# Conditional mix, attention and routed feed-forward on one core: conditions of the first tile by register loads, the routed matrix by the whole array, another load order, a gate sum ahead of a scaling, and the last product in 384 + 128 columns

## The chip, the cores and the metric

The kernel runs on one core of one Trainium2 chip. The metric is device time in microseconds (us) of one execution, the median of several runs. All data are float32 except the integer conditions and adapter numbers.

## The reference

The input `x` is 128 sequences of 32 tokens of 512 numbers. Per sequence:

```python
W  = cond_weights[condition]                  # 32x32, one of 16, chosen per sequence
h  = einsum('bct,bcd->bdt', x, W)             # mixes the 32 tokens
q, k, v = split(clip(h @ w_qkv.T, -8, 8))     # layer norm on q and on k
a  = softmax(q k^T / 4 + alibi, causal) v     # 32 heads of 16
x  = x + a @ w_out.T
u  = x @ weight[adapter].T                    # 512x512, one of 8, chosen per sequence
gate = sum(top2(u @ gate_w))                  # one number per token
y  = relu(u @ up_w)**2 @ down_w + gate * (u @ fc1_w @ expert_w @ fc2_w)
out = x + layernorm(y) * gamma + beta
```

The product `fc1_w @ expert_w @ fc2_w` does not depend on `x`.

## The kernel before, in words

Four sequences make a tile of 128 rows, so there are 32 tiles (`NTILE`). Everything is one program written out in order; a scheduler places it on the five engines, and each engine then works through its own list in order. `after(a, b)` (L130) only fixes that `a` stands behind `b`, without a wait of its own. Each DMA queue (SP's, ACT's, GpSimd's) is also worked through in order. The steps of the first tiles are written out by hand (L603 to L708); from tile 2 on a loop (L716) runs the steps of several tiles interleaved: `weigh` of tile t, `scores` of t + 1, `mix` and `project` of t + 2, and the feed-forward of the pair before.

The start. 14 products of a tile of ones (`idle`, L118 to L122) have no use but to keep TensorE busy. The conditions are loaded spread over 128 partitions (`cond_b`, L81), VectorE makes row numbers of them (`rows`, L92), and `load(t)` (L176) loads the tile `x_t` on SP's queue and gathers its condition weights `cw` row by row by an indirect DMA of GpSimd (L182). `blend` (L230) spreads `cw` into a block diagonal 128 x 128 matrix `blk` on GpSimd (L234), `mix` (L241) multiplies `x_t` with it on TensorE (`pxc`, L246), and ScalarE evicts to `xcT`. `project` (L253) multiplies `xcT` with the q, k and v weights (`wqkv_sb`, L263), which SP loads in twelve pieces (L607).

The routed matrix. `routed_inner` (L148) makes `e2 = expert @ fc2` in two halves (`pe`, L151), and `routed_outer(c)` (L157) multiplies with `fc1` into `rout_sb`, a quarter at a time. Its weights are 32 columns wide, so that four products stand side by side in the array (`pro`, L161). `rout_sb` is laid out so that partition 32 g + d of quarter c stands for row 128 g + 32 c + d.

Attention. `normalise` (L278) scales q and k on VectorE (L282), `share` (L394) divides the softmax on GpSimd (L400), `flip` (L404) transposes it to `pT` on VectorE (L408), and `weigh` (L430) multiplies `pT` with the spread values (`po`, L434). `turn_x` (L460) adds `beta` on GpSimd (L468). One line in `flip` puts the transposition of tile 2 behind the last scaling of tile 3.

Feed-forward. `load_adapters` (L192) reads the adapter numbers of a tile into registers of SP and loads its adapter weights by them (L210), `adapt` multiplies (`pad`, L484). `route` (L496) makes the gate's numbers and the routed output (`pr`, L503); VectorE takes the eight largest (`top`, L510) and adds the first two (`gs`, L512), and ScalarE scales by `gs` (L514). `up` and `down` are the feed-forward proper (L523, L537). For the very last tile `close` (L566) takes their place: it multiplies with `down_w` in two halves of 256 columns (L576), adds each half and takes its statistics on VectorE (L580, L583), then normalises and stores.

Of the kernel before, what the change touches and what calls it, by code (L numbers as in the profile page):

```python
# [11 lines left out]
F32 = mybir.dt.float32  # L12
I32 = mybir.dt.int32
AF = mybir.ActivationFunctionType
ALU = mybir.AluOpType
# [26 lines left out]
def adaln_attn_ffn(  # L42
# [27 lines left out]
    def bank(name):  # L70
        return ps.tile([P, 512], F32, tag="ps", name=name)
# [6 lines left out]


    cond_b = const.tile([P, NTILE], I32, name="cond_b")  # L80
    nc.sync.dma_start(  # L81
        out=cond_b, in_=cond.unsqueeze(1).broadcast_to([SEQ, S, NTILE])
    )
    msk = const.tile([P, SEQ + HC], F32, name="msk")
    nc.scalar.dma_start(out=msk, in_=masks)
    chan = const.tile([P, NTILE], I32, name="chan")
    for j in range(SEQ):
# [1 line left out]
            chan[j * S : (j + 1) * S, :], pattern=[[0, NTILE]], base=0, channel_multiplier=1  # L89
        )  # L90
    rows = const.tile([P, NTILE], I32, name="rows")
    nc.vector.scalar_tensor_tensor(  # L92
        out=rows, in0=cond_b, scalar=float(S), in1=chan, op0=ALU.mult, op1=ALU.add
    )
    m_seq = msk[:, 0:SEQ]
    ids = const.tile([1, B], I32, name="ids")
    wqkv_sb = const.tile([P, DC, 3 * D], F32, name="wqkv_sb")
# [20 lines left out]
    idle = hp.tile([P, GRP * P], F32, tag="act", name="idle")[:, :P]  # L118
    nc.vector.memset(idle, 1.0)
    pi = bank("pi")  # L120
    for i in range(14):
        nc.tensor.matmul(pi[:, :P], lhsT=idle, rhs=idle, start=True, stop=True)  # L122


# [11 lines left out]
        )  # L136


    exp_t = wp.tile([P, LC, LAT], F32, tag="adw", name="exp_t")
    nc.scalar.dma_start(out=exp_t, in_=expertT.rearrange("(c p) f -> p c f", p=P))  # L140
    fc2_t = wp.tile([P, LC, D], F32, tag="adw", name="fc2_t")
# [2 lines left out]
    fc1_dma = nc.sync.dma_start(out=fc1_t, in_=fc1T.rearrange("(c p) f -> p c f", p=P))  # L144
    after(fc1_dma, fc2_dma)
    e2 = w2.tile([P, LC, D], F32, tag="hT2", name="e2")

    def routed_inner(l):  # L148
        pe2 = bank(f"pe2_{l}")
# [7 lines left out]
    def routed_outer(c):  # L157
        pro = bank(f"pro_{c}")
        for l in range(LC):
            for g in range(DC):  # L160
                nc.tensor.matmul(  # L161
                    pro[ts(g, S), :],
                    lhsT=fc1_t[:, l, g * P + c * S : g * P + (c + 1) * S], rhs=e2[:, l, :],
                    start=(l == 0), stop=(l == LC - 1),
                )
        nc.scalar.copy(rout_sb[:, c, NE:], pro)

    def rstd_of(mv, n, name):
# [7 lines left out]
    def load(t):  # L176
        x_t = xp.tile([P, D], F32, tag="x", name=f"x_{t}")
        dma = nc.sync.dma_start(out=x_t, in_=x[ts(t, P), :])
        if t == 0:
            after(dma, fc1_dma)  # L180
        cw = sm.tile([P, S], F32, tag="cw", name=f"cw_{t}")
        nc.gpsimd.indirect_dma_start(  # L182
            out=cw,
            out_offset=None,
            in_=cond_w,
            in_offset=bass.IndirectOffsetOnAxis(ap=rows[:, t : t + 1], axis=0),
        )
        tiles[t] = {"x": x_t, "cw": cw}

    last_adapter_dma = []  # L190

# [38 lines left out]
    def blend(t):  # L230

        s = tiles[t]
        s["blk"] = w2.tile([P, SEQ, S], F32, tag="blk", name=f"blk_{t}")
        nc.gpsimd.tensor_tensor(  # L234
            out=s["blk"],
            in0=s["cw"].unsqueeze(1).broadcast_to([P, SEQ, S]),
            in1=m_seq.unsqueeze(2).broadcast_to([P, SEQ, S]),
            op=ALU.mult,
        )
# [38 lines left out]
    def normalise(t):  # L278
        s = tiles[t]
        r = rstd_of(s["mv"], 2, f"qk_{t}")  # L280
        for i in range(2):
            s["done"] = nc.vector.tensor_scalar(  # L282
                out=s["qk"][:, i, :], in0=s["qk"][:, i, :],
                scalar1=s["mv"][:, i, 0:1], scalar2=r[:, i : i + 1],
                op0=ALU.subtract, op1=ALU.mult,
            )

    last_flip = []
    last_pad = []
# [114 lines left out]
    def flip(t):  # L404

        s = tiles[t]
        s["pT"] = w1.tile([P, H, S], F32, tag="pT", name=f"pT_{t}")
        pT = nc.vector.transpose(  # L408
            out=s["pT"].rearrange("p h q -> p (h q)"),
            in_=s["s"].rearrange("p h k -> p (h k)"),  # L410
        )
        if t == GRP:
            after(pT, tiles[t + 1]["done"])

    def spread(t):

# [79 lines left out]
    def route(t, half):  # L496

        s = tiles[t]
        hT = pairs[t // GRP]["hT"]
        n = ROUT[half + 1] - ROUT[half]  # L500
        pr = bank(f"pr_{t}_{half}")
        for c in range(DC):
            nc.tensor.matmul(  # L503
                pr[:, :n], lhsT=hT[:, c, ts(t % GRP, P)],
                rhs=rout_sb[:, c, ROUT[half] : ROUT[half + 1]],
                start=(c == 0), stop=(c == DC - 1),
            )
        if half == 0:
            top = sm.tile([P, 8], F32, tag="top", name=f"top_{t}")
            nc.vector.max(out=top, in_=pr[:, :NE])  # L510
            s["gs"] = sm.tile([P, 1], F32, tag="gs", name=f"gs_{t}")
            nc.vector.tensor_tensor(out=s["gs"], in0=top[:, 0:1], in1=top[:, 1:2], op=ALU.add)  # L512
# [53 lines left out]
    def close(t):  # L566

        s = tiles.pop(t)
        y, n = s["y"], D // 2
        banks = [bank(f"pd_{t}_{h}") for h in range(2)]  # L570
        st = sm.tile([P, H], F32, tag="mx", name=f"stf_{t}")[:, :12].rearrange(
            "p (h n) -> p h n", h=2
        )
        for h in range(2):
            for f in range(FC):
                nc.tensor.matmul(  # L576
                    banks[h][:, :n], lhsT=pairs[t // GRP]["acts"][f][:, ts(t % GRP, P)],
                    rhs=down_sb[:, f, ts(h, n)], start=(f == 0), stop=(f == FC - 1),
                )
            nc.vector.tensor_tensor(  # L580
                out=y[:, ts(h, n)], in0=y[:, ts(h, n)], in1=banks[h][:, :n], op=ALU.add
            )
            nc.vector.bn_stats(out=st[:, h], in_=y[:, ts(h, n)])  # L583
        mv = sm.tile([P, 1, 2], F32, tag="mv1", name=f"mvf_{t}")
        nc.vector.bn_aggr(out=mv[:, 0, :], in_=st)
        r = rstd_of(mv, 1, f"f_{t}")
        for h in range(2):
            nc.vector.scalar_tensor_tensor(
                out=y[:, ts(h, n)], in0=y[:, ts(h, n)], scalar=mv[:, 0, 0:1],
                in1=gam_sb[:, ts(h, n)], op0=ALU.subtract, op1=ALU.mult,  # L590
            )
        for h in range(2):
            nc.vector.scalar_tensor_tensor(
                out=y[:, ts(h, n)], in0=y[:, ts(h, n)], scalar=r,
                in1=s["x"][:, ts(h, n)], op0=ALU.mult, op1=ALU.add,
            )
            (nc.sync, nc.scalar)[h].dma_start(
                out=out[ts(t, P), ts(h, n)], in_=y[:, ts(h, n)]
            )

    load(0)  # L603
    for cols in ((0, 1), (2,)):
        for c in range(DC):
            for i in cols:
                dma = nc.sync.dma_start(  # L607
                    out=wqkv_sb[:, c, ts(i, D)], in_=w_qkvT[c * P : (c + 1) * P, ts(i, D)]
                )
                after(dma, fc1_dma)  # L610
    load(1)
    for l in range(LC):
        routed_inner(l)
    blend(0)
    blend(1)
    mix(0)
    routed_outer(0)
# [222 lines left out]
```

## Time and profile before

| | us |
|---|---|
| median of 3 runs (1243.22 to 1243.87) | 1243.75 |
| the profiled execution, whole | 1243.48 |
| its span, first to last instruction | 1241.7 |
| busy: GpSimd (POOL) | 431.3 |
| busy: ScalarE (ACT) | 327.6 |
| matmuls of the q, k, v products (L263), 768 records | 340.3 |
| matmuls of the routed matrix (L151 and L161), 8 and 64 records | 3.7 and 7.5 |
| matmuls of the last product (L576), 32 records | 7.1 |
| matmuls of ones (L122), 28 records | 5.3 |

One execution is profiled, and times in it count from its first instruction. An engine's busy time is the union of its instructions; a matmul's end is modelled, so that consecutive ones overlap. Each float32 matmul stands as two records. PE is TensorE's multiplication, PEld its weight load, DVE is VectorE, ACT is ScalarE, POOL is GpSimd, SP issues DMAs; a q behind an engine's name is its queue of instructions that only issue or wait. In a line such as `pxc L246 <- POOL blk L234` the engine's instruction on line 246 waited for GpSimd's on line 234.

### The profile page before, as it was taken

What the parts mean: (1) busy time and instruction counts of PE and PEld (TensorE: products, weight loads), DVE (VectorE), ACT (ScalarE), POOL (GpSimd) and SP (SyncE); (2) the same over time, 40 slices, a digit from 0 to 9 for tenths busy, and PEclk for the clock granted to TensorE, in tenths of its full rate; (3) what the DMA queues carried; (4) which work ended last, traced back from release to release, by engine and by line L of the source; (5) the groups of instructions that cost most, each with busy time, mean ns of one, the idle gap of its engine ahead of it and who ended that gap; (6) DMA issues with size and microseconds to landing.
All of it is one profiled execution on the core that took longest, in us unless ns stands there. A gap on an engine that the chain in (4) does not pass through costs nothing.

```text
span 1241.7 us, 28016 instructions
## 1 busy us (share of the span) xinstructions
PE 1231.8 (99%) x11676; PEld 793.6 (64%) x11676; DVE 656.8 (53%) x1086; ACT 327.6 (26%) x648; POOL 431.3 (35%) x393
## 2 busy tenths in 40 slices
PE   9999999999999999999999999999999999999997
PEld 5476566674666756567665666746667565675765
DVE  2874654646456364563645546465564646636222
ACT  2433223222222313233132232222322222231211
POOL 4444333333433424234243333333333242342410
PEclk9999999999999999999999999999999999999999
DMA  9745554435545355543445444455353554533620
GB/s 312 212 163 188 204 194 149 152 122 204 205 160 169 117 178 196 184 175 135 146 180 205 180 153 136 147 204 204 141 177 108 189 204 169 181 113 143 214 109 18
DMA packets 93380, 209.23 MB, mean 169 GB/s; under 512 B 11717, under 2 KB 42438, under 8 KB 93254
## 3 DMA queue, kind: packets, MB, share of 16 engines
q1 hardware_dynamic: 89270, 198.65, 45.8%
q0 software_dynamic: 3424, 8.39, 1.9%
q8 instruction: 92, 1.51, 0.5%
q10 hardware_dynamic: 560, 0.40, 0.1%
q14 instruction: 34, 0.28, 0.1%
HBM read 176.47 MB, written 30.93 MB: 167 GB/s over the span
## 4 chain that ended last, share of the span: by engine, by line
PE 97%; DVE 1%; DMA 1%; issue 0%; POOL 0%; SPq 0%; DVEq 0%
PE pqkv L263 26%; PE pu L523 18%; PE pd L537 17%; PE pr L503 9%; PE pad L484 9%; PE pw L454 9%; PE psc L366 3%; PE po L434 3%; PE pxc L246 2%; PE pro L161 1%; PE pd L576 1%; DMA adw<-in_adapt_w 0%; DVE qk L282 0%; POOL cw L182 0%; PE pt L317 0%
## 5 line engine op out<-in xcount | busy, mean ns | idle before, releaser
L263 PE MATMUL pqkv<-wqkv_sb,xcT 128*128 128x512 f32 x768 | 340.3, 592 | 0.0
L263 PEld LDWEIGHTS pqkv<-wqkv_sb,xcT 128*128 128x128 f32 x768 | 145.3, 190 | 169.1 <-issue 162.9
L523 PE MATMUL pu<-hT,up_sb 128*128 128x256 f32 x1024 | 228.7, 379 | 0.0
L537 PE MATMUL pd<-down_sb,act 128*128 128x512 f32 x496 | 220.4, 592 | 0.0
L523 PEld LDWEIGHTS pu<-hT,up_sb 128*128 128x128 f32 x1024 | 193.5, 190 | 32.6 <-issue 6.9
L342 DVE TENSOR_TENSOR kx<-T_qk,m_half 128x512 f32<-128x512 f32 x128 | 107.4, 897 | 106.5 <-ACT T_qk L338 106.5
L537 PEld LDWEIGHTS pd<-down_sb,act 128*128 128x128 f32 x496 | 93.2, 190 | 104.7 <-issue 103.6
L421 POOL TENSOR_TENSOR vx<-v,msk 128x1024 f32<-128x1024 f32 x64 | 126.7, 2004 | 60.4 <-DVE v L269 49.9
L529 POOL TENSOR_TENSOR act<-act 128x256 f32<-128x256 f32 x128 | 78.1, 615 | 166.7 <-ACT act L528 165.7
L503 PE MATMUL pr<-rout_sb,hT 128*128 128x256 f32 (+1 forms) x512 | 125.8, 389 | 0.0
L484 PE MATMUL pad<-adw,T_x 128*32 128x128 f32 x4096 | 119.9, 273 | 0.5 <-issue 0.4
L387 POOL TENSOR_TENSOR s<-s,mx 128x1024 f32<-128x1024 f32 x32 | 61.2, 1914 | 157.0 <-DVE top L510 146.2
L454 PE MATMUL pw<-wout_sb,aT 128*128 128x512 f32 x256 | 115.2, 592 | 0.0
L503 PEld LDWEIGHTS pr<-rout_sb,hT 128*128 128x128 f32 x512 | 94.7, 190 | 32.0 <-issue 19.9
L484 PEld LDWEIGHTS pad<-adw,T_x 128*32 128x32 f32 x4096 | 111.4, 110 | 3.3 <-issue 2.1
L397 DVE TENSOR_REDUCE den<-s 128x32 f32<-128x1024 f32 x32 | 39.0, 1220 | 100.5 <-ACT s L392 97.0
L468 POOL TENSOR_TENSOR x<-x,bet_sb 128x512 f32<-128x512 f32 x32 | 40.9, 1279 | 144.8 <-DVE blocks_x L298 144.8
L454 PEld LDWEIGHTS pw<-wout_sb,aT 128*128 128x128 f32 x256 | 48.6, 190 | 60.6 <-issue 60.0
L528 ACT ACTIVATE act<-pu 128x256 f32<-128x256 f32 x128 | 47.2, 379 | 140.9 <-PE pu L523 140.9
L564 POOL DMA_DIRECT2D out<-y x30 | 18.0, 601 | 180.2 <-DVE y L560 93.1
L400 POOL TENSOR_TENSOR s<-s,rden 128x1024 f32<-128x1024 f32 x32 | 61.5, 1921 | 50.7 <-DVE rden L399 47.8
L251 ACT COPY xcT<-pxc 128x512 f32<-128x512 f32 x32 | 18.7, 585 | 201.6 <-PE pxc L246 200.2
(75 smaller groups left out, 1100.5 us busy)
## 6 DMA issues: line engine op xcount, KB each, us to landing
adw<-in_adapt_w SPq DMA_DIRECT2D x256, 512.0 KB
away_qk<-blocks_qk SPq DMA_DIRECT2D x28, 512.0 KB
T_qk<-away_qk SPq DMA_DIRECT2D x112, 128.0 KB
x<-in_x SPq DMA_DIRECT2D x32, 256.0 KB
away_x<-blocks_x SPq DMA_DIRECT2D x30, 256.0 KB
T_x<-away_x SPq DMA_DIRECT2D x120, 64.0 KB
out<-y POOLq DMA_DIRECT2D x30, 256.0 KB, 2.9
wqkv_sb<-in_w_qkvT SPq DMA_DIRECT2D x12, 256.0 KB
```

Source lines behind the costliest of these rows:

```text
L263: nc.tensor.matmul(s["pp", i], lhsT=s["xcT"][:, c, :], rhs=wqkv_sb[:, c, ts(i, D)], start=(c == 0), stop=(c == DC - 1),)
L342: kx = nc.vector.tensor_tensor(out=s["kx"][:, c], in0=k[:, :, c].unsqueeze(2).broadcast_to([P, SEQ, HQ, S]), in1=m_half.unsqueeze(1).unsqu ...
L387: nc.gpsimd.tensor_tensor(out=s["s"], in0=s["s"], in1=mx.unsqueeze(2).broadcast_to([P, H, S]), op=ALU.subtract,)
L400: nc.gpsimd.tensor_tensor(out=s["s"], in0=s["s"], in1=rden.unsqueeze(2).broadcast_to([P, H, S]), op=ALU.mult)
L421: nc.gpsimd.tensor_tensor(out=vx, in0=s["v"][:, ts(half, D // 2)].rearrange("p (h d) -> p h d", d=HD).unsqueeze(2) .broadcast_to([P, H // ...
L454: nc.tensor.matmul(pw, lhsT=s["aT"][:, g].rearrange("p b q -> p (b q)"), rhs=wout_sb[:, g, :], start=(g == 0), stop=(g == 3),)
L484: last_pad[:] = [nc.tensor.matmul(pad[ts(g, S), ts(j, P)], lhsT=s["xT"][:, j, c], rhs=s["adw"][c // 2][j][:, c % 2, ts(g, P)], start=(c == ...
L503: nc.tensor.matmul(pr[:, :n], lhsT=hT[:, c, ts(t % GRP, P)], rhs=rout_sb[:, c, ROUT[half] : ROUT[half + 1]], start=(c == 0), stop=(c == DC ...
L523: nc.tensor.matmul(pu[:, : GRP * P], lhsT=up_sb[:, c, ts(f, P)], rhs=pair["hT"][:, c, :], start=(c == 0), stop=(c == DC - 1),)
L528: nc.scalar.activation(a, pu[:, : GRP * P], AF.Relu)
L529: nc.gpsimd.tensor_tensor(out=a, in0=a, in1=a, op=ALU.mult)
L537: nc.tensor.matmul(s["pd"], lhsT=pairs[t // GRP]["acts"][f][:, ts(t % GRP, P)], rhs=down_sb[:, f, :], start=(f == 0), stop=(f == FC - 1),)
```

## The change

Five things change.

1. The conditions of tile 0 are read as four numbers (`cid`) by a small DMA on ScalarE's queue, loaded into registers of ScalarE, and each of the four 32 x 32 blocks is fetched by a plain DMA whose address comes from a register. The other tiles keep the indirect gather; that of tile 1 stands behind the first `blend`.
2. `cond_b` and `rows` come after the first loads: SP's queue now begins with `fc2`, `fc1`, `x_0`, then `cond_b`, then the q, k and v weights. `blend(0)` is written ahead of `load(1)`.
3. `fc1` is regrouped by two copies on VectorE (`fc1_r`), so that `routed_outer` takes weights 128 columns wide. 9 products of ones take the place of 14.
4. For tile 0 the gate sum `gs` stands ahead of both scalings of tile 3, and `flip` of tile 2 behind both.
5. `close` multiplies 384 columns and then 128, with statistics per 128 columns.

On the engines' lists this also moves two things by the scheduler's choice: the load of `down_sb` now stands behind the adapter loads of tile 1, and the load of `x_6` stands after the first exchange of q, k and x through memory.

```diff
-    nc.sync.dma_start(
-        out=cond_b, in_=cond.unsqueeze(1).broadcast_to([SEQ, S, NTILE])
-    )
...
-    for i in range(14):
+    for i in range(9):
         nc.tensor.matmul(pi[:, :P], lhsT=idle, rhs=idle, start=True, stop=True)
...
+    cid = sm.tile([P, H], I32, tag="mx", name="cid")
+    nc.scalar.dma_start(out=cid[0:1, 0:SEQ], in_=cond[:, 0:1].rearrange("s a -> a s"))
...
+    fc1_r = w1.tile([P, H, S], F32, tag="pT", name="fc1_r").rearrange(
+        "p (l e g) d -> p l e g d", l=LC, e=DC
+    )
+    for l in range(LC):
+        nc.vector.tensor_copy(
+            out=fc1_r[:, l],
+            in_=fc1_t[:, l, :].rearrange("p (g e d) -> p e g d", g=DC, e=DC),
+        )
...
-            for g in range(DC):
-                nc.tensor.matmul(
-                    pro[ts(g, S), :],
-                    lhsT=fc1_t[:, l, g * P + c * S : g * P + (c + 1) * S], rhs=e2[:, l, :],
-                    start=(l == 0), stop=(l == LC - 1),
-                )
+            nc.tensor.matmul(
+                pro,
+                lhsT=fc1_r[:, l, c].rearrange("p g d -> p (g d)"), rhs=e2[:, l, :],
+                start=(l == 0), stop=(l == LC - 1),
+            )
...
+        if t == 0:
+
+            _, regs = nc.values_load_multi_w_load_instructions(
+                cid[0:1, 0:SEQ], engines=[mybir.EngineType.Activation],
+                min_val=0, max_val=cond_w.shape[0] // S - 1,
+            )
+            for j in range(SEQ):
+                nc.scalar.dma_start(
+                    out=cw[ts(j, S), :],
+                    in_=cond_w.rearrange("(n s) k -> n s k", s=S)[ds(regs[j], 1)].rearrange(
+                        "a s k -> (a s) k"
+                    ),
+                )
+            return
...
         if t == GRP:
-            after(pT, tiles[t + 1]["done"])
+            for scaling in tiles[t + 1]["norm"]:
+                after(pT, scaling)
...
+            if t == 0:
+                for scaling in tiles[3]["norm"]:
+                    after(scaling, gs)
...
-        for h in range(2):
+        for lo, hi in ((0, DC - 1), (DC - 1, DC)):
+            cols = slice(lo * P, hi * P)
+            pd = bank(f"pd_{t}_{lo}")[:, : (hi - lo) * P]
             for f in range(FC):
                 nc.tensor.matmul(
-                    banks[h][:, :n], lhsT=pairs[t // GRP]["acts"][f][:, ts(t % GRP, P)],
-                    rhs=down_sb[:, f, ts(h, n)], start=(f == 0), stop=(f == FC - 1),
+                    pd, lhsT=pairs[t // GRP]["acts"][f][:, ts(t % GRP, P)],
+                    rhs=down_sb[:, f, cols], start=(f == 0), stop=(f == FC - 1),
                 )
-            nc.vector.tensor_tensor(
-                out=y[:, ts(h, n)], in0=y[:, ts(h, n)], in1=banks[h][:, :n], op=ALU.add
-            )
-            nc.vector.bn_stats(out=st[:, h], in_=y[:, ts(h, n)])
+            nc.vector.tensor_tensor(out=y[:, cols], in0=y[:, cols], in1=pd, op=ALU.add)
+            for c in range(lo, hi):
+                nc.vector.bn_stats(out=st[:, c], in_=y[:, ts(c, P)])
...
     load(0)
+    first = nc.sync.dma_start(
+        out=cond_b, in_=cond.unsqueeze(1).broadcast_to([SEQ, S, NTILE])
+    )
+    after(first, tiles[0]["dma"])
+    nc.vector.scalar_tensor_tensor(
+        out=rows, in0=cond_b, scalar=float(S), in1=chan, op0=ALU.mult, op1=ALU.add
+    )
...
+    blend(0)
     load(1)
     for l in range(LC):
         routed_inner(l)
-    blend(0)
     blend(1)
```

More of the change, by code (lines that the diff above doesn't have):

```diff
@@ L91, in adaln_attn_ffn @@
     rows = const.tile([P, NTILE], I32, name="rows")
-    nc.vector.scalar_tensor_tensor(
-        out=rows, in0=cond_b, scalar=float(S), in1=chan, op0=ALU.mult, op1=ALU.add
-    )
     m_seq = msk[:, 0:SEQ]
@@ L181, in load @@
         cw = sm.tile([P, S], F32, tag="cw", name=f"cw_{t}")
-        nc.gpsimd.indirect_dma_start(
+        tiles[t] = {"x": x_t, "cw": cw, "dma": dma}
+        if t == 0:
[11 more added lines that the diff above has]
+            return
+        gather = nc.gpsimd.indirect_dma_start(
             out=cw,
@@ L187, in load @@
         )
-        tiles[t] = {"x": x_t, "cw": cw}
+        if t == 1:
+            after(gather, tiles[0]["blend"])
     last_adapter_dma = []
@@ L233, in blend @@
         s["blk"] = w2.tile([P, SEQ, S], F32, tag="blk", name=f"blk_{t}")
-        nc.gpsimd.tensor_tensor(
+        s["blend"] = nc.gpsimd.tensor_tensor(
             out=s["blk"],
@@ L281, in normalise @@
         for i in range(2):
-            s["done"] = nc.vector.tensor_scalar(
+            done = nc.vector.tensor_scalar(
                 out=s["qk"][:, i, :], in0=s["qk"][:, i, :],
@@ L286, in normalise @@
             )
+            s.setdefault("norm", []).append(done)
     last_flip = []
@@ L511, in route @@
             s["gs"] = sm.tile([P, 1], F32, tag="gs", name=f"gs_{t}")
-            nc.vector.tensor_tensor(out=s["gs"], in0=top[:, 0:1], in1=top[:, 1:2], op=ALU.add)
+            gs = nc.vector.tensor_tensor(
+                out=s["gs"], in0=top[:, 0:1], in1=top[:, 1:2], op=ALU.add
+            )
+            if t == 0:
+                for scaling in tiles[3]["norm"]:
+                    after(scaling, gs)
             s["y"] = w2.tile([P, D], F32, tag="y", name=f"y_{t}")
@@ L569, in close @@
         y, n = s["y"], D // 2
-        banks = [bank(f"pd_{t}_{h}") for h in range(2)]
-        st = sm.tile([P, H], F32, tag="mx", name=f"stf_{t}")[:, :12].rearrange(
-            "p (h n) -> p h n", h=2
-        )
-        for h in range(2):
+        st = sm.tile([P, H], F32, tag="mx", name=f"stf_{t}")[:, : 6 * DC].rearrange(
+            "p (c n) -> p c n", c=DC
+        )
+        for lo, hi in ((0, DC - 1), (DC - 1, DC)):
+            cols = slice(lo * P, hi * P)
+            pd = bank(f"pd_{t}_{lo}")[:, : (hi - lo) * P]
             for f in range(FC):
                 nc.tensor.matmul(
-                    banks[h][:, :n], lhsT=pairs[t // GRP]["acts"][f][:, ts(t % GRP, P)],
-                    rhs=down_sb[:, f, ts(h, n)], start=(f == 0), stop=(f == FC - 1),
-                )
-            nc.vector.tensor_tensor(
-                out=y[:, ts(h, n)], in0=y[:, ts(h, n)], in1=banks[h][:, :n], op=ALU.add
-            )
-            nc.vector.bn_stats(out=st[:, h], in_=y[:, ts(h, n)])
+                    pd, lhsT=pairs[t // GRP]["acts"][f][:, ts(t % GRP, P)],
+                    rhs=down_sb[:, f, cols], start=(f == 0), stop=(f == FC - 1),
+                )
+            nc.vector.tensor_tensor(out=y[:, cols], in0=y[:, cols], in1=pd, op=ALU.add)
+            for c in range(lo, hi):
+                nc.vector.bn_stats(out=st[:, c], in_=y[:, ts(c, P)])
         mv = sm.tile([P, 1, 2], F32, tag="mv1", name=f"mvf_{t}")
@@ L603, in adaln_attn_ffn @@
     load(0)
+    first = nc.sync.dma_start(
[4 more added lines that the diff above has]
+        out=rows, in0=cond_b, scalar=float(S), in1=chan, op0=ALU.mult, op1=ALU.add
+    )
     for cols in ((0, 1), (2,)):
@@ L609, in adaln_attn_ffn @@
                 )
-                after(dma, fc1_dma)
+                after(dma, first)
+    blend(0)
     load(1)
```

## The prediction

> **What bounds the kernel now.** I read the page's first part, then the list of what TensorE waited for, then the chain of work that ended last, and only then the timeline at the two ends. The page:
>
> ```profile
> PE 1231.8 (99%) x11676; PEld 793.6 (64%) x11676; DVE 656.8 (53%) x1086; ACT 327.6 (26%) x648; POOL 431.3 (35%) x393
> ```
>
> TensorE is busy for 1231.8 of 1241.7 us, so only its start, its end, its few waits and its own instructions can give time. Its waits, whole list (waiter, line, releaser: us in total, times, longest):
>
> ```profile
> PE pi L122 <- DVE idle L119: 1.1, 1, 1.1
> PE pxc L246 <- POOL blk L234: 0.9, 1, 0.9
> PE po L434 <- DVE gs L512: 0.6, 1, 0.6
> PE pad L484 <- issue: 0.4, 1, 0.4
> ```
>
> Besides these 3.0 us there is the tail: the last matmul ends at 1235.0, leaving 6.7. The chain at the start (start us, us, what):
>
> ```profile
> 10.52 0.41 POOL blk L234
> 10.93 0.04 issue
> 10.97 1.16 PE pxc L246 x8
> 12.13 1.85 PE pro L161 x16
> 13.98 7.06 PE pqkv L263 x16
> ...
> 33.12 3.57 PE pro L161 x32
> ...
> 37.77 1.85 PE pro L161 x16
> ```
>
> To see: TensorE starts the first tile (pxc, from 10.97) when GpSimd has spread its condition weights (blk). What went before, from the timeline (start us, us, engine, line):
>
> ```profile
> 1.08 5.26 PE L122 MATMUL pi<-idle 128*128 128x128 f32 x28 [1.08 <-DVE idle L119]
> ...
> 2.52 0.16 DVE L126 TENSOR_TENSOR m_half<-msk 128x4 f32<-128x4 f32 x1 [1.49 <-DMA msk<-in_masks]
> ...
> 4.12 0.19 DVE L92 SCALAR_TENSOR_TENSOR rows<-cond_b,chan 128x32 int32<-128x32 int32 x1 [1.44 <-DMA cond_b<-in_cond]
> 4.60 1.17 POOL L182 DMA_INDIRECT cw<-in_cond_w,rows  x1 [2.55 <-DVE rows L92]
> ...
> 6.39 3.67 PE L151 MATMUL pe<-fc_t,exp_t 128*128 128x512 f32 x8
> ```
>
> A float32 matmul is two records. Counted by windows of 1 us, the fillers (L122) run 6 to 7 records per us up to 5 us and 11 from 5 to 6: the array doubles its speed at about 5.0, although the page's clock column says 9 throughout.
>
> **The change, part by part** (times in the old execution's clock).
>
> *Start of pe.* Nine fillers are 18 records: 0.37 for the first, then 0.2135 each (from the 6 to 7 per us): 1.08 + 0.37 + 17 x 0.2135 = 5.1. So the filler no longer holds pe, and its operands decide. By the windows, DMA moved 5, 71, 151, 381, 377 KB in the microseconds from 1 on: full rate (some 0.38 MB/us) is reached only at 4. What must be through for pe is masks 6, cond_b 16, exp_t 262 and fc2 524 KB, 808 together, at 5.5; pe starts at 6.39, so landing costs up to 0.8. In the new order fc2 leads SP's queue: its issue moves from 1.57 to 0.77, and cond_b's small rows (0.77 to 4.12, the slowest transfer here for its size) no longer go before it. exp_t is issued about 0.3 later, behind the new cid load (ids, the like row, took 0.26 to issue). Bounds for pe: 5.1 (fillers) to 6.39 (no better than now). I take 5.3: fc2 0.8 earlier would give 5.6, and the idle engine time between 2 and 4 us lets both come a little sooner.
>
> *Conditions.* cid is issued at 1.17. masks is the nearest row: issue 0.76, user at 2.52, 1.76. So cid is in by 2.9. Register loads are shown on SP: TENSOR_LOAD at 19.08, first adapter load at 20.88, 1.8 for four values; then 0.55 per load (three in 1.44, each 0.33). On ACT: first load 4.7, fourth 6.35. Landing: 1.76 by the masks row, 3.3 by cond_b's, which competes with bulk loads as these will. I take 1.8, since these are 4 KB over 32 rows each; fourth in at 8.15, then 0.41 for blk (L234): 8.6, or 10.1 at the far end. The gather it replaces was issued at 4.60 and used at 10.52, so a wait of that kind, 5.9, is what is removed.
>
> *pxc.* pe occupies 3.5 us of issue (3.67 less the drain): 5.3 + 3.5 = 8.8. blk at 8.6 is just ahead. I take 8.9 against 10.97: **-2.07**. What is late next: ACT's table load (1.28, at 1.65 now) falls behind the four loads, to 6.7 to 8.0; the first copy of pe, due at 8.38 - 1.1 = 7.3, slips to 8.0, the second ends at about 9.6; pro wants it at 10.0. Covered by 0.4.
>
> *Weights.* In the new order each SP load waits for the load eight before it, and the eight q/k weight loads now wait among others for the four condition loads (third, fifth, sixth, eighth). By bytes the eight are through at 13.1 now; TensorE wants the eighth at 13.98 + 7 x 0.86 = 20.0, or 17.9 after the change. If the eighth is issued at 8.2, behind some five others of 0.69 us each (256 KB at 0.38 MB/us), it lands by 12 to 13. Cost 0, cover 5 us. The other gathers start on POOL only after blk, at 8.6; the second was used 5.9 after the first's issue, tile 1 wants it 10 later. Nothing. cond_b and rows likewise.
>
> *Routed matrix.* Each routed_outer was 16 narrow records (four side by side) in 1.85 or 3.57 for two; it becomes 4 full ones. A 512-column record costs 6.87/16 = 0.429, so 1.72 and 3.43. Gain 0.13 + 0.14 + 0.13 = **-0.40**. The two DVE copies that regroup fc1 (512 columns, at most 0.69 each as an eviction of that size) lie at 6 to 7.5, where DVE is busy 0.5 us in 14.
>
> *Gate sum.* Now:
>
> ```profile
> 80.39 3.10 DVE L282 TENSOR_SCALAR qk<-qk,mv,rstd_qk 128x512 f32<-128x512 f32 x2
> 83.41 0.16 DVE L510 MAX8 top<-pr 128x8 f32<-128x8 f32 x1
> 83.50 1.22 DVE L408 STREAM_TRANSPOSE pT<-s 128x1024 f32<-128x1024 f32 x1
> 84.64 0.11 DVE L512 TENSOR_TENSOR gs<-top 128x1 f32<-128x1 f32 x1
> ```
>
> The list names gs, but po multiplies pT, which ends at 84.72; gs only ended last. The two scalings take 3.10 here and 1.00 at 25.09. The difference is GpSimd: L400 from 79.88 to 81.79 and L468 from 81.75 to 83.20. After the change max and gs come first, at 81.3 (pr ends at 81.2), and the scalings start at 81.6. Without the neighbour they would end at 82.6, pT at 83.8, and the whole wait of 0.6 would go. The Trainium skill, "SBUF — State Buffer", section "Who interferes with whom", says that a VectorE op in a 2-port mode and a GpSimd op exclude each other for a whole instruction, in issue order. By that the first scaling again gets in at 81.79, the second again after 83.20, and pT only gains the slot of max: 0.08. The row agrees (second scaling over 0.29 after L468's end). I take the lock: **-0.08**; bounds -0.6 and +0.1 (if L468 gets in before both).
>
> *Tail.* Columns cost the same: 16 x 0.322 + 16 x 0.111 = 6.93 for 32 x 0.2155 = 6.90, +0.03. After the last matmul the chain is
>
> ```profile
> 1235.08 0.43 DVE y L580
> ...
> 1235.54 0.44 DVE stf L583
> ```
>
> Add and statistics cost 0.42 and 0.43 at 256 columns, 0.69 and 0.69 at 512, so about 0.29 each at 128: -0.27. bn_aggr over four groups: +0.02. The wide part needs 0.59 + 3 x 0.33 = 1.58 on DVE, under the 1.78 of the last matmuls. Together **-0.22**.
>
> *SP's order later.* down_sb (2 MB, 5.5 us) is issued at 41.3 now and goes behind tile 1's adapters (issued from 72.4, 4.2 MB): through by about 93, wanted at 127; adapters for tile 2 are issued at 93.25. One x load moves ahead of T_x (0.7 us; T_x is wanted 4 later). Cost 0.
>
> Sum: -2.07 - 0.40 - 0.08 - 0.22 = **-2.77**. On the profiled execution (1243.48 = span 1241.73 and 1.75 around it) that is 1240.7; it lies 0.27 under the median, so for the median 1243.75: **1241.0**.
>
> **Rivals.**
> 1. *The conditions are late* (landing by cond_b's row): blk at 10.1, pxc at 10.15; 1.25 of the gain goes: 1242.2. For it: bulk loads hold the engines from 4 us on; against it: masks' 1.76. 25%.
> 2. *The clock gate* (ends slower). The Trainium skill, "TensorE: Matmul & The Clock Gate", section "Part 1: The HAM clock gate", says that the array runs at half speed until a free-running window of about 3.4 us has been busy throughout, so that the switch moves from run to run. Here it came 3.9 after the first filler; nine fillers end 0.1 after that, and TensorE then waits 0.2. By the row alone the cost is nothing; by the rule with a switch 0.5 later, (5.5 - 5.3)/2 = 0.1; if the gap spoils one window, it comes at 5.0 + 2 x 3.4 = 11.8 and costs (11.8 - 5.3)/2 = 3.3: 1244.3, slower. It decides once the switch comes after 5.3 + 2 x 2.77 = 10.8. Since 14 fillers hid such shifts and nine do not, 5% for this, 7% for a part of it (1242.5).
> 3. *Better*: pe at 5.1 and conditions ahead, or the whole of po's wait gone: 1240.3. 10%.
> 4. *The change doesn't do what it says*: loads on ACT could wait for exp_t (the fourth does, by its semaphore). It lands by 5.2, the load is due at 6.35: nothing. Counted in 1.
>
> **Numbers.** The sum as it stands, 53%: 1240.4 to 1241.7. A measurement here can tell about 0.2%, 2.5 us, from no change; the border is 1241.26, inside that case, so most of it, case 3 and little else make faster: 0.58. Same: the rest of it, case 1, the part of case 2: 0.37. Slower: 0.05. Range 1240.2 to 1242.5.
>
> **What would show it.** Chain: pe at 5.3, pxc at 8.9 with no wait over 0.2 on blk, pqkv at 11.8; four pro groups of 1.72; po's wait still 0.5; after the last matmul two DVE steps of 0.29. Wrong if pxc waits for blk, if fewer than 9 matmul records per us run after 5.1, or if pqkv waits for a weight.

## The result, and the profile after

The changed kernel takes 1248.51 us (median of 6 runs, 1247.69 to 1249.9) against 1243.8 for the kernel before in the same session: a ratio of 1.0039, 95% interval 1.0026 to 1.0052. It is slower by 4.7 us, where 2.8 less was forecast. The profiled execution took 1248.46, its span is 1246.7. The changed file has its own line numbers: `pe` is L158, `pxc` L268, `pqkv` L285, `po` L458, `pad` L508, `psc` L389, `pr` L527.

The page, TensorE's busy time and one of its DMA queues (packets, MB, share):

```profile
PE 1234.0 (99%) x11618; PEld 794.6 (64%) x11618; DVE 656.2 (53%) x1090; ACT 327.4 (26%) x648; POOL 429.3 (34%) x392
...
q8 instruction: 92, 1.51, 0.5%
```

58 records fewer are executed, and yet TensorE is busy 2.2 us longer. The second line, passed over in the prediction, is TensorE's instructions being fetched, and turns out to matter most. What TensorE waited for, from the whole list:

```profile
PE pad L508 <- issue: 3.0, 3, 2.4
PE pe L158 <- DMA exp_t<-in_expertT: 2.2, 1, 2.2
...
PE po L458 <- DVE pT L431: 0.5, 1, 0.5
```

Two waits are new, one of 2.2 us before `pe` and one of 2.4 inside `pad`, the latter for nothing that the profile names. `pxc` does not wait for `blk`, but only because `pe` is later still. The chain at the start:

```profile
2.49 4.79 DMA exp_t<-in_expertT
7.28 0.04 issue
7.33 5.40 PE pe L158 x8
12.72 0.89 PE pxc L268 x8
13.62 1.72 PE pro L167 x4
15.34 3.00 PE pqkv L285 x7
```

`pe` starts at 7.33 (6.39 before, 5.3 forecast) and takes 5.40 in place of 3.67; `pqkv` starts 1.36 later than before. The chain at tile 1, first in the kernel before, then in the changed one:

```profile
85.96 3.49 PE pad L484 x128
89.46 1.09 PE psc L366 x64
```

```profile
87.32 3.01 PE pad L508 x106
90.33 2.45 issue
92.78 0.86 PE pad L508 x22
93.64 1.89 PE psc L389 x64
```

106 records run, TensorE stands still for 2.45 us in the middle of a group, the other 22 run, and `psc` (of tile 3, which follows the `pad` of tile 1) takes 1.89 where it took 1.09. Windows (busy us of TensorE with its records, granted clock, DMA share, GB/s) show why both products are slow:

```profile
8.00:9.00 1.00, 1.00 (x3) 0.60 0.76 179
10.00:11.00 1.00, 1.00 (x3) 0.50 0.10 12
...
92.00:96.00 4.00, 3.22 (x88) 0.69 0.48 178
```

The granted clock is 0.50 from 8.19 to 11.61 and from 93.53 to 96.94, each time 3.41 us, each time after a long wait. At the end:

```profile
1241.06 0.30 DVE y L610
...
1241.38 0.30 DVE stf L612
...
1241.71 0.28 DVE mvf L614
```

Two steps of 0.30 took the place of 0.43 and 0.44. From the last product to the end of VectorE's work it is 2.31 against 2.60.

The distance between equal products of the two traces tells where the time went. `psc` of tile 2 starts 0.92 later than before; `pr` of tile 0 1.16; `po` of tile 2 1.36; the last quarter of `pad` of tile 1 4.13; `po` of tile 3 5.68; `pr` of tile 1 6.35; the last product 6.06. Behind the last product VectorE is done 0.29 sooner and the span ends another 0.8 sooner: 5.0 in the span. Those 0.8 are no accident of this trace. From the last product to the end of the span it is 5.6 us in all fifteen traces of kernels with the last product in 384 + 128 (all of them have the routed matrix by the whole array too), and 6.7 in the five without. Why the end comes sooner is not shown.

### The profile page after: what moved, and what is told of

Same layout as the page of the kernel before. It is cut to its first block, busy times and chain, and to the rows that moved or that the text cites. A ratio compares the mean times of both kernels' runs of the same rounds, so it can differ in the third digit from the quotient of the medians.

```text
span 1246.7 us, 27931 instructions
## 1 busy us (share of the span) xinstructions
PE 1234.0 (99%) x11618; PEld 794.6 (64%) x11618; DVE 656.2 (53%) x1090; ACT 327.4 (26%) x648; POOL 429.3 (34%) x392
## 4 chain that ended last, share of the span: by engine, by line
PE 98%; DVE 1%; DMA 0%; issue 0%; ACTq 0%; DVEq 0%
PE pqkv L285 26%; PE pu L552 18%; PE pd L566 17%; PE pr L527 9%; PE pad L508 9%; PE pw L478 9%; PE psc L389 3%; PE po L458 3%; PE pxc L268 2%; PE pro L167 1%; PE pd L606 1%; PE pe L158 0%; DMA exp_t<-in_expertT 0%; PE pt L340 0%; DVE qk L304 0%
## 5 line engine op out<-in xcount | busy, mean ns | idle before, releaser
L285 PE MATMUL pqkv<-wqkv_sb,xcT 128*128 128x512 f32 x768 | 340.1, 592 | 0.0
L285 PEld LDWEIGHTS pqkv<-wqkv_sb,xcT 128*128 128x128 f32 x768 | 145.4, 190 | 168.7 <-issue 163.3
L566 PEld LDWEIGHTS pd<-down_sb,act 128*128 128x128 f32 x496 | 93.2, 190 | 104.7 <-issue 103.6
L527 PE MATMUL pr<-rout_sb,hT 128*128 128x256 f32 (+1 forms) x512 | 125.8, 389 | 0.0
L508 PE MATMUL pad<-adw,T_x 128*32 128x128 f32 x4096 | 120.7, 273 | 3.1 <-issue 3.0
L508 PEld LDWEIGHTS pad<-adw,T_x 128*32 128x32 f32 x4096 | 111.6, 110 | 6.4 <-issue 5.4
L527 PEld LDWEIGHTS pr<-rout_sb,hT 128*128 128x128 f32 x512 | 94.7, 190 | 32.0 <-issue 20.3
```

The costliest lines, as they stand in the source:

```text
L285: nc.tensor.matmul(s["pp", i], lhsT=s["xcT"][:, c, :], rhs=wqkv_sb[:, c, ts(i, D)], start=(c == 0), stop=(c == DC - 1),)
L508: last_pad[:] = [nc.tensor.matmul(pad[ts(g, S), ts(j, P)], lhsT=s["xT"][:, j, c], rhs=s["adw"][c // 2][j][:, c % 2, ts(g, P)], start=(c == ...
L527: nc.tensor.matmul(pr[:, :n], lhsT=hT[:, c, ts(t % GRP, P)], rhs=rout_sb[:, c, ROUT[half] : ROUT[half + 1]], start=(c == 0), stop=(c == DC ...
L566: nc.tensor.matmul(s["pd"], lhsT=pairs[t // GRP]["acts"][f][:, ts(t % GRP, P)], rhs=down_sb[:, f, :], start=(f == 0), stop=(f == FC - 1),)
```

## Experiments

Every kernel here computes the whole reference. Times are medians beside runs of the kernel before on the same chip in the same session; a trace is of one execution, and its time is given where it lies far from the median.

### 1. What makes pad wait

The first theory was the moved load of `down_sb`: 2 MB directly behind the adapter loads of tile 1, which share the DMA engines with it. In the changed kernel it was put back to its old place, and in the kernel before moved behind the adapters:

```diff
+    down_dma = nc.sync.dma_start(out=down_sb, ...)
     load_adapters(1, tiles[2]["psc"])
+    after(tiles[1]["adma"], down_dma)      # first adapter load of tile 1
```

> The changed kernel with the load of down_sb put back ahead of tile 1's adapter loads. Theory A: the wait of 2.45 us at pad of tile 1 is the last adapters sharing the DMA engines with the 2 MB of down_sb that now stand right behind them, and the half-speed stretch after it (granted clock 0.69 and 0.88 from 92 to 100 us) is a consequence of that wait. Then the wait and the low clock there go together: from po to the next pqkv the new kernel lost 5.68 - 1.36 = 4.3, so about 1244.2. Rival B: the adapters are late by themselves (their eight issues took 5.85 us in place of 4.26 and began 1.2 later); then a wait of 1 us or more stays, and the time is 1246 or more. Rival C: the low clock there has nothing to do with the wait; then about 1246 (only the 2.45 gone).

> The kernel before, with the load of down_sb put behind tile 1's adapter loads and nothing else on purpose (the two x loads that followed them come ahead of them). Theory A (shared DMA engines): pad of tile 1 now waits 2 to 2.5 us and the clock dips behind it; up to 4.3 slower, about 1247.5 to 1248. Rival B (adapters late by themselves in the changed kernel only): pad waits less than 0.5, 1243.8.

Measured: 1246.4 (before: 1243.66; ratio 1.0019, 1.0011 to 1.0026) and 1246.48 (1.0026, 1.0018 to 1.0034). Neither theory stood. With `down_sb` out of the way `pad` still waits 1.6 us (in the trace, of the slowest of 15 runs, 1249.05), at a time when the DMA engines are nearly idle (share 0.08 from 92 to 96), so it waits for no adapter. And in the kernel before, the moved load makes not `pad` wait, but `psc`:

```profile
PE psc L366 <- issue: 2.2, 1, 2.2
```

`psc` needs no adapter either. A third run, meant for the clock, gave the clue: the kernel before with nothing changed but 9 products of ones in place of 14.

```diff
-    for i in range(14):
+    for i in range(9):
```

> The kernel before with 9 products of ones in place of 14. They end at 5.1, and pe starts when fc2 is in, at about 6.2: a gap of 1.1. Theory A1 (a gap has to be long, since the 0.9 us that the kernel before waits for blk left the clock at 1.00): the clock stays up, pe takes 3.7, nothing changes, 1243.8. Theory A2 (any gap at this place spoils the clock): pe takes 5.4 and ends at 11.6 to 11.8, pxc starts 0.7 later than at 10.97 and runs slower: 1244.5 to 1245.

Measured: 1247.47 (1.0027, 1.0018 to 1.0037), single runs from 1244.5 to 1249.3. `pe` ran at full clock and `pxc` even came 0.24 earlier. The loss is 80 us later, on the same chain:

```profile
85.91 1.70 PE pad L484 x58
87.61 2.14 issue
89.75 2.17 PE pad L484 x70
```

Five idle products at the start end long before tile 1, so their number is what I suspected. Queue q8, of the kind instruction, moves 92 packets of 16,384 bytes in both kernels. The changed kernel's TensorE has 11,618 weight loads, 11,618 products and 293 other records in its list, 23,529 / 92 = 256 a packet, near enough: by its size q8 carries TensorE's instructions. A product of ones is four instructions, so nine fillers shorten the list by 20, and the changed kernel (58 records fewer, each with its load) by 116 ahead of tile 1. Counted in order, the long stops of the traces (nine of over 1 us without a releaser, in eight kernels) come behind 706, 1729 or 1730, and 1985 to 1987 records: each time 193 to 195 more than a multiple of 256, and behind the start so do all the shorter ones over 0.2 us. With pieces that end at 194, all of them stand at the end of a piece:

| kernel | piece ends, in | next fetch begins | following piece used up | TensorE goes on |
|---|---|---|---|---|
| before | 82.1, `pr` | 78.5 | 87.1 | at once |
| nine fillers | 83.6, `pt` | 87.3 | 87.6 | 89.8 |
| changed | 86.8, `po` | 90.4 | 90.3 | 92.8 |
| changed, `down_sb` back | 89.7, `po` | 92.6 | 93.2 | 94.8 |
| before, a piece later | 87.1, `pad` | 87.2 | 90.1 | at once |
| the same, `down_sb` behind | 87.1, `pad` | 89.9 | 90.3 | 92.5 |

I read it so: the end of a piece sets off the fetch of the piece after the next, for there is one packet for each end, and where it is late TensorE stops one piece further on. Among long products the fetch begins before the array gets to the end (78.5 for 82.1), as if the sequencer, which hands out the instructions, were some us ahead of it. `po`, `pad` and `psc` are 512 instructions in 5.7 us, so a piece lasts about 3 us. The last two rows differ only in the load in flight: with the adapters through (the DMA share falls at 86.5) the fetch began 0.1 after the end of its piece, with `down_sb` on the engines 2.8. In the four rows that stop it began 2.8 to 3.7 after, and TensorE went on 2.2 to 2.6 after it began. The Trainium skill, "Runtime: NRT & Kernel Launch", section "Instruction fetch mechanics", has the blocks of 256 instructions, and calls the cost of crossing one mostly hidden; the traces agree with the size, and 2.45 us in the changed kernel is not hidden.

### 2. The count alone

If that is right, the count of instructions decides, whatever the idle products take. So the count was restored with products of 32 columns, meant to take less time than the fillers left out, and once the list was shifted by exactly one piece (64 products):

```diff
-    for i in range(14):
+    for i in range(9):
         nc.tensor.matmul(pi[:, :P], lhsT=idle, rhs=idle, start=True, stop=True)
+    for i in range(5):
+        nc.tensor.matmul(pi[:, :32], lhsT=idle, rhs=idle[:, :32], start=True, stop=True)
```

and, for the whole piece, in place of the second loop

```diff
+    for i in range(69):
+        nc.tensor.matmul(
+            pi[ts(i % DC, S), :S], lhsT=idle[:, :S], rhs=idle[:, :S], start=True, stop=True
+        )
```

> The kernel before with 9 products of ones of 128 columns and 5 of 32 columns: the time of the fillers is that of the run with 9 (which was 3.8 slower), the number of TensorE instructions that of the kernel before. Theory F (instruction fetch): TensorE's instructions come in pieces of 256 (16 KB) by a DMA queue of their own; nine fillers shift every piece by 20 instructions, so that the request for a piece falls among the adapter loads and the short products of tile 1 run out of instructions. With the count restored the waits at pad and psc of tile 1 go, and the time is 1243.7 (within 0.5). Rival G (idle TensorE at the start): the gap of about 1.5 us before pe is what costs; it is nearly as long here, so 1246 or more.

> The kernel before with 9 products of ones of 128 x 128 and 69 of 32 x 32 in place of 14: TensorE's list is longer by 64 products, 256 instructions, one whole piece. Theory F with pieces of 256: the ends of pieces fall on the same products of tile 1 as in the kernel before, so pad and psc wait for nothing, though the list is shifted thirteen times further than by the nine fillers alone. The small products end at 7.5 to 9, so pe and pxc come 0.5 to 2 later: 1243.5 to 1245.5. Rival (any shift of the list costs, or the waits come from elsewhere): waits of 1.5 to 3 us at pad or psc, 1246 to 1248.

Measured: 1243.53 against 1243.05 (1.0002, 0.9994 to 1.0011): the 3.8 us are gone. This run alone does not rule out the rival of the idle time, since the five narrow products took as long as wide ones and `pe` did not wait at all. Later runs do: with the count restored TensorE stood idle for 1.0 us (1243.74 run of part 4) and 2.4 us (1242.7 run) before `pe`, and nothing waited long at `pad` or `psc`; with 19 fillers it was not idle there, and `pad` waited 2.45. With 69 small products 1250.58 (1.0056, 1.004 to 1.0071), out of the range expected, but not for tile 1. Its whole list of waits:

```profile
PE pi L124 <- issue: 3.6, 9, 0.5
PE pi L122 <- DVE idle L119: 1.1, 1, 1.1
PE po L438 <- DVE gs L516: 0.6, 1, 0.6
```

`pad` and `psc` wait for nothing. The distance to the kernel before is 7.75 us from the first tile on and 7.70 after tile 1: all of the loss is in the start, where the small products stopped nine times by 0.2 to 0.5 us and the clock fell to half. Why they stop there is open.

### 3. The routed matrix without its side effect

Two parts of the change alone, the whole-array `routed_outer` and the last product in 384 + 128, on the kernel before; then with 9 wide and 29 narrow products of ones, so that the 96 instructions that the routed matrix loses are made up.

> The kernel before with two parts of the change alone: the routed matrix by the whole array, and the last product in 384 + 128. By the sums of the prediction it gains 0.40 + 0.22: 1243.1. Theory F: the routed matrix takes 96 instructions out of TensorE's list ahead of tile 1 and the pieces of 256 move against the short products; the fetch then falls among the adapter loads, with waits of 1.5 to 3 us at po, pad or psc of tile 1 as in the changed kernel: 1245 to 1247. Rival: no such waits, 1243.1.

> The same two parts, with 9 products of ones of 128 columns and 29 of 32 columns in place of 14, so that TensorE's number of instructions ahead of tile 1 is that of the kernel before. Theory F: no waits at pad and psc; the gains of 0.40 and 0.22 are left, 1243.1, less up to 0.2 if pe comes earlier. Rival (the waits have another cause, the time of each step or the DMA's order): like the run without the narrow products.

Measured: 1249.1 and 1251.81 against 1243.05, both spoilt by the edit itself. In the first, the two copies of `fc1` stood ahead of `rows` on VectorE and waited for `fc1` until 7.6, so the gather went out at 8.8 and `pxc` waited 5.0 for `blk`. In the second, the products of 32 columns took as long as wide ones, 12.2 us for 58 records at half clock. Still, `pad` waited 1.4 in the first and not at all in the second. Mended, with the copies behind `rows`, and with products whose weights are 32 columns as well (11 wide, 27 small):

```diff
+        copy = nc.vector.tensor_copy(out=fc1_r[:, l], ...)
+        after(copy, rows_op)
```

> The kernel before with the routed matrix by the whole array and the last product in 384 + 128, as in the earlier run of these two parts, but with the two regrouping copies of fc1 kept behind rows on VectorE, so that the first gather is not held up. Both theories: blk at 10.5 again, the 5.0 us wait for it gone. Theory F (instruction fetch): TensorE has 96 instructions fewer ahead of tile 1, a piece of 256 ends at po of tile 2 and its successor is asked for while the adapters load, so pad or psc of tile 1 wait 1 to 2.5 us: 1244.3 to 1246. Rival: no such wait, the gains of 0.40 and 0.22 alone: 1242.9.

> The same, with 11 products of ones of 128 x 128 and 27 of 32 x 32 in place of 14 of 128 x 128: TensorE's number of instructions ahead of tile 1 is that of the kernel before. The narrow products used so far took as long as wide ones, since they loaded the same 128 weights; those of po, 32 weights wide, take 17 ns a record, so 54 records should take 0.9 to 1.8 us and end at 6.5 to 7.3. Theory F: no waits at pad and psc, 0.40 + 0.22 gained: 1242.9 (1243.4 if the small products hold pe up to 7.3 and pxc with it). Rival: like the run without them.

Measured: 1246.92 (1.0032, 1.002 to 1.0044) and 1242.39 (0.9995, 0.9988 to 1.0001) against 1243.02. The first waits at `psc` of tile 1 (at 53.3) and at `pad` of tile 1:

```profile
PE psc L375 <- issue: 2.6, 1, 2.6
PE pad L493 <- issue: 1.4, 1, 1.4
```

and has the clock at half for 3.41 us behind the first of them. The second waits there for 0.2 at most, so the count of instructions is worth 4.5 us, although its `pxc` starts 1.1 later. That its 0.6 under the kernel before equals the forecast 0.62 is luck: `pxc` is 1.0 late, the routed matrix takes back 0.67, and the end 1.1.

### 4. The start and the clock

> The changed kernel with 19 products of ones in place of 9, enough to keep TensorE busy until exp_t lands at 7.3. Theory A: the clock fell to 0.5 from 8 to 12 because TensorE stood idle for 2.2 us before pe; with the idle time filled pe takes 3.7 in place of 5.4 and ends at 11.0, then pxc waits for blk (11.7) and starts 0.8 earlier than in the changed kernel: about 1247.7. Rival B: the clock falls there for another reason (the first real products, or a count from the start); then pe still takes 5.4 and the time is 1248.5.

Measured: 1247.13 (1.0033, 1.002 to 1.0046). The clock rose late in this run, at 6.55, so the 19 products of ones lasted to 8.0; `pe` took 3.6, and the clock did not fall again. `pxc` starts at 11.7, and `pxc` of tile 1 then waits 1.0 for `x_1`, which the changed kernel is late enough not to notice.

The changed kernel with the count restored, `down_sb` in its old place in all but the last:

> The changed kernel with down_sb ahead of tile 1's adapter loads, and 29 products of ones of 32 columns behind the nine of 128: TensorE's number of instructions ahead of tile 1 is that of the kernel before, and most of the 2.2 us before pe is filled. Theory F with the gap theory of the clock: no waits at pad and psc, the clock stays at 1.00 from 7 to 12, pe from 7.4 to 11.0, pxc at 11.75 behind blk (0.8 later than before), then the gains of routed matrix, gate sum and tail (0.70): 1243.9. If the clock still falls: 1245 to 1246. Rival (waits at pad have another cause): 1246.4 as with down_sb alone moved, less the start.

> The changed kernel with down_sb ahead of tile 1's adapters, and 29 products of ones of 32 x 32 behind the nine: the count of instructions is that of the kernel before, and the fillers end by 6.1 to 7. Theory F: no waits at pad and psc. Then pe from 7.35; if a gap of about 1 us leaves the clock up, pe ends at 11.0, pxc follows blk at 11.75, and the time is 1243.75 + 0.8 - 0.7 = 1243.9; if small products don't count as work for the clock, pe takes 5.4 to 6.6, pxc starts at 12.7 to 14 and the time is 1245 to 1246.5.

> The changed kernel with 29 products of ones of 32 x 32 behind the nine and nothing else: the count of instructions of the kernel before, down_sb still behind tile 1's adapters. If the load of down_sb delays the fetch of instructions, as in the kernel before with that load moved, psc of tile 1 waits about 2.2 and the time is 2 to 2.5 over the same kernel with down_sb in its old place (1243.74): 1246. If it doesn't, 1243.7. If the last adapters themselves are late, pad waits for a DMA by name.

Measured: 1250.26 against 1243.05 with 29 products of 32 columns, which hold `pe` up to 14.4 (no wait at `pad` or `psc`). With 29 small products of 32 x 32, 1243.74 against 1243.02 (1.0006, 0.9997 to 1.0014), near the 1243.9 expected, on the chain:

```profile
87.11 3.49 PE pad L513 x128
90.61 1.09 PE psc L394 x64
```

With `down_sb` left behind the adapters, 1247.75 against 1243.39: `psc` waits 2.3, its fetch begins 3.0 after the end of its piece (0.2 in the 1243.74 run), and the clock falls for one window after an idle 1.91 before `pe`. So over the kernel before it is 4.7 for the changed kernel, 4.4 with the count restored, 2.7 with `down_sb` back, and 0.7 with both: neither alone mends it. Some 4.0 go with the two together, the clock among them. In the trace of the 1243.74 run `psc` of tiles 0 to 2 is 0.95 to 1.05 late from the start, and `po` of tile 2 0.20 more; the end takes 1.1 of that back.

Two runs on the start, both with the count restored. In the first `exp_t` is issued ahead of `cid` on ScalarE's queue; in the second `cond_b` leads SP's queue again as in the kernel before (11 wide, 27 small products, gate sum in its old place):

> The same with the gate sum as changed, and exp_t issued ahead of cid on ScalarE's queue. Theory: exp_t goes out at 1.25 in place of 2.49 and pe starts at about 6.3 in place of 7.3, without a gap; cid goes out 0.4 later, blk at 11.6 to 12 decides pxc, and the load of x_1 (behind the weights that wait for the condition blocks) then makes tile 1's mix wait as before: 1243.7, no gain. Rival: pe's start decides, and pxc starts near 10: 1242.

> The changed kernel with the load order of the kernel before (cond_b leads SP's queue, then fc2, fc1, x_0, the weights), the gate sum in its old place, down_sb in its old place and the count of instructions restored by 27 small products behind 11 wide ones; kept are the register loads, the routed matrix and the last product. Theory (SP's bulk loads delay ScalarE's): masks lands at 2.5 again and cid by about 4, exp_t is no longer last and pe starts at 6.4 to 7; the register chain of 1.7, the issues of 1.8 and the landing of 1.7 put blk at 9 to 9.5, so pe decides pxc at 10.1 to 10.6: 0.4 to 0.9 ahead of the kernel before, with 0.65 from the other parts: 1.1 to 1.5 under it, near 1242.0. Rival (cid's four separate elements are slow by themselves): cid still lands at 6 and blk at 11.3: no better than the kernel before less 0.3.

Measured: 1246.48 against 1243.39, and 1242.7 against 1242.85 (1.0, 0.9992 to 1.0008). Issued at 1.24, `exp_t` still landed at 7.1, hardly before the 7.3 of the issue at 2.49. That trace is of one of the fastest of 14 runs, 1244.23, with one window at half clock behind the idle time before `pe`; what cost the median 2.3 more it does not show. With `cond_b` ahead (the trace is of the fastest run, 1241.39), `masks` was in by 2.4 (4.2 in the changed kernel), the first condition block was issued at 5.09 (7.77), but now `exp_t`, issued at 2.44 behind `cid`, was last:

```profile
PE pe L166 <- DMA exp_t<-in_expertT: 2.4, 1, 2.4
```

`pe` began at 8.14 and `pxc` at 11.68. `cid` was in by 3.4, 1.0 after its issue ended. The fourth condition block was issued only at 8.11, since by its semaphore it waits for `exp_t`: the prediction's fourth rival, which did not bite in the changed kernel. So SP's bulk loads do hold up ScalarE's, the four elements of `cid` are slow to issue (1.20) and not to land, and `exp_t` behind them is late.

### 5. The gate sum

The order of before in `flip` and `route`, else as the 1243.74 run:

> The changed kernel with down_sb in its old place, the count of instructions restored, and the gate sum and both scalings in the order of the kernel before. Theory: the new order puts max and the sum, which wait for pr, ahead of both scalings, so that pT ends later; undoing it takes back the 0.20 that po of tile 2 had lost: 1243.5. Rival: it gained the forecast 0.08: 1243.8. The trace decides (start of po of tile 2 less start of psc of tile 2: 13.65 in the kernel before, 13.85 with the new order).

Measured: 1244.19 against 1243.39, which tells nothing of 0.2 us. The trace does: the distance to the kernel before is 0.64 from `psc` of tile 0 through `po` of tile 2, without the step of 0.20.

### 6. A version that beats both

The kernel before with routed matrix, last product and count as in 3, and the first tile's `blk` directly behind its own gather:

```diff
+    blend(0)
     load(1)
...
+        if t == 1:
+            after(gather, tiles[0]["blend"])
```

> The kernel before with the routed matrix, the last product in 384 + 128 and the count of instructions restored as above, and with the first tile's blk right behind its own gather on GpSimd, ahead of the three gathers that stood before it (no register loads, the load order of the kernel before). blk should follow the landing of the first gather (issued 4.6 to 5.8, landing about 2 later), at about 8.2, so that pe (6.4 to 10.05) decides and pxc starts at 10.1 in place of 10.97: 0.85 gained beside 0.62: 1242.2 and faster than both kernels. Rival: the gather lands only at 10 (bulk loads in its way) and nothing is gained by the order, 1242.9; or the second gather's later issue makes tile 1 wait.

> The best version once more: the kernel before with the routed matrix, the last product in 384 + 128, the count of instructions restored and blk behind its own gather. Expected 1.1 under the kernel before, as it was; if the register loads pay once the load order is the old one, the other run of this pair is at or under it.

Measured: 1241.86 (0.999, 0.9984 to 0.9997) and 1241.23 (0.9985, 0.9978 to 0.9993), 1.2 and 1.6 under the kernel before: small, but clear of 1 in both. The order on GpSimd itself gained little, as its rival had it: the gather ended issuing at 5.8 and `blk` ran only at 10.4 and 10.2.

## Why the prediction was wrong, step by step

The forecast was -2.77, the traces show +5.0 in the span. By the distances above, 3.4 of these 7.8 us lie in the start up to `po` of tile 0 (+0.92 for -2.07 - 0.40), 5.2 in the stops at ends of pieces and the half clock behind them, up to `pr` of tile 1, which the sum had at nothing, 0.3 in the gate sum, and the end gave 0.8 more than forecast; the little that is left falls in the long middle.

*Start of pe: wrong.* "So the filler no longer holds pe" was right, the fillers end at 5.1; "I take 5.3" failed. The bytes were counted as those of `masks`, `cond_b`, `exp_t` and `fc2`, but `fc1` and `x_0`, issued at 1.26 and 1.76, go ahead of `exp_t`, issued at 2.49. 1.57 MB at 0.39 MB/us are 4.0 us, and `exp_t` landed last: `fc2` at 4.5, `fc1` at 5.9, `x_0` at 6.6, `exp_t` at 7.3. The bound "no better than now" was no bound.

*Conditions: wrong at one link.* `cid` was to be in by 2.9, by the `masks` row of a run in which SP's first load was small and slow. It came at 6.0, and `masks` itself at 4.2. Its issue took 1.20, not the 0.26 of `ids`. The rest held: 1.67 from register load to first block (1.8), four issues in 1.84 (1.65), landing 1.7 (1.8).

*pxc: -2.07 became +1.6,* its first product at 12.56. The start was then partly given back: `psc` of tile 0 is 1.0 late. The next thing late, `x_1`, was not in the list "what is late next": its load stands behind weights that wait for the condition blocks, and in the four runs that wait for it the `pxc` of tile 1 starts at 21.7 to 22.7. "Cost 0, cover 5 us" held for the weights, not for what is queued behind them.

*Clock gate: the rival of 5% happened,* though not by its price. The clock did rise as the filler ended, and fell for one window after a gap of 2.22 us; `pe` lost 1.7. The step that failed is the length of the gap, forecast at 0.2. Windows of 3.41 us do fit every change of the clock in the traces, but a window need not be busy throughout for the clock to rise, as the prediction has it: it rose after one with 0.64 us idle (the 1243.74 run).

*Routed matrix: right in size* (1.72, 3.43, 1.91), *and with the fewer fillers the step that failed most.* "Gain 0.13 + 0.14 + 0.13" counted TensorE's time and not its list. Ninety-six instructions fewer, and 20 with the fillers, moved every piece behind them. No part of the sum had the fetch, and q8 on the page was not read.

*Gate sum: wrong sign,* +0.20 for -0.08, outside the bounds. The step that failed is "the first scaling again gets in at 81.79". The changed kernel's VectorE and GpSimd:

```profile
81.36 0.15 DVE L179 RECIPROCAL rstd_qk<-std_qk 128x2 f32<-128x2 f32 x1
82.41 0.17 DVE L534 MAX8 top<-pr 128x8 f32<-128x8 f32 x1 [0.90 <-PE pr L527]
82.62 0.35 DVE L536 TENSOR_TENSOR gs<-top 128x1 f32<-128x1 f32 x1
82.89 2.03 DVE L304 TENSOR_SCALAR qk<-qk,mv,rstd_qk 128x512 f32<-128x512 f32 x2
...
81.04 1.91 POOL L423 TENSOR_TENSOR s<-s,rden 128x1024 f32<-128x1024 f32 x1 [2.87 <-ACT std_qk L177]
82.91 1.27 POOL L492 TENSOR_TENSOR x<-x,bet_sb 128x512 f32<-128x512 f32 x1
```

In the kernel before the scalings stood ready from 80.39; GpSimd's second operation took 1.45 there, and the pair ended 0.29 after it. Now `max` waits for `pr`, the sum takes 0.35 beside GpSimd where it took 0.11 and ends as GpSimd's first operation does, the second takes its usual 1.27, and the pair ends 0.74 after it. It looks as if neither scaling got in ahead of the second operation; that is read from these times, and no run varied it. From the end of the reciprocal to `pT` it is 3.41 against 3.21. The wait of `po` stayed 0.5, as said, but says nothing of when `po` starts.

*Tail: right in its terms,* 0.29 less behind the last product and 0.04 more in it, -0.25 for -0.22. But the end of the span comes 0.8 sooner still, in every trace with this tail. No term had that.

*SP's later order: wrong.* "Cost 0" asked when `down_sb` is wanted, and not what flows beside it: alone, in the kernel before, it made `psc` wait 2.2 and cost 2.8.

## What to carry to other kernels

An edit that changes the number of an engine's instructions moves every later fetch of them: when a gain in products comes back as a loss far away, look for waits on nothing inside a dense group of short instructions, and count to the end of a piece. Where dense groups run beside bulk loads, hold the count fixed (a few small products at the start did it, for 4.5 us in the kernel before), and keep bulk loads away from them (in the changed kernel it took both, for 4.0), before judging an edit. And what a load costs is decided by all that is in flight with it, not by its place in its own queue.

## What the runs showed of the hardware that was not expected

- *Fetch.* TensorE went on 2.2 to 2.6 us after a late fetch began. The packet itself took 1.0 to 1.4 in the rows of the table. That the engines' load delays its beginning rests on two pairs that differ in the place of `down_sb` alone (0.1 and 2.8 us in the kernel before, 0.2 and 3.0 in the changed one with the count restored). Load alone is not enough: in the kernel before a fetch began 0.7 after the end of its piece, at 53.7, with the DMA share at 1.04 to 0.99. The mechanism is open.
- *Clock.* Idle time of 2.22 and 2.45 us inside one window of 3.41 halved the clock for the next window; the same 2.45 split over two windows as 1.99 and 0.46 (the run with 19 fillers) did not. An idle 1.91 and an idle 1.73 did, where 0.7 of small products went before them in the window; an idle 1.62 behind as many did not.
- *Narrow products.* 32 columns with 128 x 128 weights take 0.21 us a record at half clock, no less than 128 columns, and in the run with 29 of them on the kernel before the clock stayed at half until 20.1 with TensorE busy throughout. With 32 x 32 weights a record takes 12 to 20 ns, but when many follow each other TensorE stopped for 0.4 to 0.5 us after every four or five records for a while in two of the runs and not in the others; why is open.
